# Two-layer graph network: where the joins of DMA-transposed features, tile 24's transposes and the last tile's TensorE transposes stand in their queues

## The chip, the cores and the metric

The kernel runs on one core of a Trainium2 chip. The metric is the device time of one execution in microseconds. Each core has a matrix engine (TensorE, "PE" in the profile, with its weight loads listed as "PEld"), a vector engine (DVE), a scalar engine (ACT), a general engine (POOL, GpSimd), and a queue that issues transfers (SP). POOL and ACT can issue transfers too. The engines run side by side; each takes its own instructions in the order in which they are queued, and they wait for one another through semaphores.

## The reference

The input is `x` (3327 nodes by 1024 features) and a weighted adjacency matrix `adj` (3327 by 3327). Two layers follow each other:

```python
# layer 0: quantised graph convolution
h = relu(layernorm(x))
support = relu(act_quant(h) @ weight_quant(w0))          # then quantised again
x = x + adj @ act_quant(support)                         # up to scales
# layer 1: graph attention with 8 heads of 64 features
h = relu(layernorm(x))
Wh = h @ W                                               # 1024 -> 8 x 64
e = leaky_relu(e_src[:, None] + e_dst[None, :])          # e_src = Wh.a1, e_dst = Wh.a2
att = softmax(where(adj > 0, e, -9e15))                  # per head, over neighbours
h = elu(att @ Wh)
x = x + mlp(h)                                           # four dense layers, relu between
```

## The kernel before

The nodes are padded to 26 tiles of 128 (`T` = 26). Five stages follow one another on TensorE.

**Supports** (up to about 126 us): layer 0's quantised products, left in SBUF as 26 tiles `s_int`.

**Aggregation** (about 126 to 904 us, the loop at L798). For each tile `t` of output rows, 26 column tiles of the transposed adjacency are multiplied with `s_int`. To keep float32 accuracy with two single-pass products, each piece is split: ACT copies the rounded high part (`hi`, L191), DVE subtracts it from the original (`lo`, L195) and writes the mask byte (`mk`, L196). The 26 column tiles come in seven parts (`PARTS`: five of four tiles, two of three). `at`, `hi` and `lo` have three buffers each, so a split waits until PE has finished with the part three places earlier. A generator, `columns`, emits the loads and splits two parts ahead of the products: when the loop is at part `n` of tile `t`, the latest split emitted is part `n + 2`, which for `n` = 5 is the first part of the next tile.

When a tile's products are done, ACT takes them out of PSUM (`y`, L845, held in the name `emptied`), DVE scales them (L846, `resumed`), adds `x`, takes the layer norm's statistics and writes the normalised `y` (L150). Then the features have to be transposed for `Wh = h @ W`. `transposed_by_dma` (L613) splits the float32 words into 16-bit halves: ACT packs half of the columns (`yh`, L622), a DMA transpose on SP's queue turns them (`yht`, L624), and the same again for the other half. These two transfers are called planes. Then ACT puts the 16-bit halves together again, one copy for each plane (`ht`, L628, the list `joins`). The next adjacency row's first load and the next `x` tile are issued on SP behind the last plane (`issue_after(turned.ins)`, L186 and L801).

Every second tile multiplies the transposed features of two earlier tiles, `t - 2` and `t - 1`, with the head weights. Seven half-size products (L702) are combined by additions (Strassen's scheme); `combined` (L666) makes the sums before them on DVE at part 3 and `pair_of_heads` (L686) threads the products in between those of parts 5 and 6. `closing_of_heads` (L763) then makes scores and features: score sums on DVE, `ratio` and two `ft` exponentials on ACT (L776, L780), the feature product on DVE (L781), and the feature's split into three bfloat16 terms `fw` (ACT L785, DVE L786, ACT L787, DVE L788). `fw` has one buffer; it is written to `feat_d` in HBM by POOL's queue (L791). `rows_of_scores` (L746) transposes the source scores and sends them to `src_d`. The engines' queues are ordered by a scheduler from the program; `queue_behind(a, b)` (L155) puts `a` behind `b` there without a semaphore.

**Hand-over** (about 904 to 962 us). The last two tiles have no pair of their own in the loop. Tile 24 goes through `heads` (L731), eight matmuls on the DMA-transposed `ht`, with its output in the one `sp` bank of PSUM, taken out by ACT (`wht`, L743). Tile 25 is transposed by PE itself (`transposed_by_tensor`, L637): two groups of four transposes, "turns", both into the one PSUM bank `last`, each taken out by an ACT copy (L648). Both tiles keep their own features for head 0 in SBUF (`own`, L790, `f_even`). The attention's first groups are threaded in between by the list `turn` (L1060).

**Attention** (to about 1876 us). For each head and each of four node ranges, ACT makes `over` (L953: is source plus destination score positive), DVE turns it with the mask into two fp8 selections `sel` (L962, L963), and PE sums the features over all 26 tiles (`acc`, L982). The 13 pairs of tiles form seven groups (`GROUPS`); pair 6 has its `over` from DVE. `over` has two buffers, `sel` six; selections are made two groups ahead. The score row `srow` (L917), masks (L908) and features (L902) come by SP's queue.

**Dense layers** end the kernel, the first of them threaded into the last attention row.

The lines of the hand-over that are changed read:

```python
        queue_behind(planes[0], load_src(0))
        with tc.issue_after(turned.ins):
            ins = load_features(0, range(8))
        ...
        queue_behind(joins[0], ends["scalar"])
        queue_behind(joins[1], joins[0])
        queue_behind(emptied, joins[1])
        queue_behind(resumed, ends["vector"])
        select(1)
        turn = [(of_k[-1], turns[0][0]), (turns[-1][1], last_of_k[0]), (last_of_k[-1], None)]
```

Here `planes`, `joins`, `emptied` and `resumed` hold what the last pass through them left: the planes and joins of tile 24, `y` and its scaling of tile 25. `ends` are the first and last ACT instruction and the last DVE instruction of the first selection.

Of the kernel before, what the change touches and what calls it, by code (L numbers as in the profile page):

```python
# [67 lines left out]
def two_layer_kernel(  # L68
# [23 lines left out]
    nc = tc.nc  # L92
# [81 lines left out]
    with tc.tile_pool(name="at", bufs=2, reuse_waits="tile") as atp:  # L174
# [3 lines left out]
        def adjacency(t, js, mk, turned):  # L178
# [11 lines left out]
            hi = atp.tile([P, PN, P], F32R, tag="hi", name="hi", bufs=3)[:, :nj]  # L190
            ins = nc.scalar.copy(hi, at)  # L191
            if t == 0:
# [8 lines left out]
            if js is PARTS[-1]:  # L201
                if t == T - 1:
                    nc.vector.memset(mk[:, :, rows_of(t) :], EDGE)
                nc.gpsimd.dma_start(mask_d[t], mk)
            return hi, lo, mk

        def adjacencies():
            for t in range(T):
                mk = None
                for js in PARTS:  # L210
                    hi, lo, mk = adjacency(t, js, mk, turned)
                    yield hi, lo
# [383 lines left out]
        with tc.tile_pool(name="differences", bufs=1, reuse_waits="tile") as dp, tc.tile_pool(  # L596
# [16 lines left out]
            def transposed_by_dma(y, t):  # L613
# [6 lines left out]
                for c in range(FC):  # L620
# [3 lines left out]
                    planes.append(nc.sync.dma_start_transpose(yht, yh.rearrange("p two f -> p (two f)")))  # L624
                    parts.append(yht)
                for c, yht in enumerate(parts):
                    joins.append(
# [6 lines left out]
                    )  # L634
                return ht, planes[-1]

# [25 lines left out]
            def weight_differences():  # L662
                for d, one, other in ((t3, b22, b12), (b12, b12, b11), (t2, b22, b12), (t4, b21, t2)):
                    nc.vector.tensor_tensor(d, one, other, ALU.subtract)
# [133 lines left out]
            for t in range(T):  # L798
# [6 lines left out]
                for n, js in enumerate(PARTS):  # L805
# [7 lines left out]
                    if t == 1 and n == 0:  # L813
                        weight_differences()
                    if paired and n == 3:
                        of = combined(t - 2)
# [35 lines left out]
                if t == T - 1:  # L852
                    break
                ht, turned = transposed_by_dma(y, t)
                hts[t], scales[t] = ht, r
# [25 lines left out]
    with tc.tile_pool(name="over", bufs=2, reuse_waits="tile") as overp, tc.tile_pool(  # L881
# [156 lines left out]
        load_mask(0, slice(0, TH), nc.gpsimd)  # L1038
        queue_behind(planes[0], load_src(0))
        with tc.issue_after(turned.ins):  # L1040
            ins = load_features(0, range(8))
        with tc.issue_after(ins.ins):
# [11 lines left out]
        ends = select(0)  # L1054
        queue_behind(joins[0], ends["scalar"])
        queue_behind(joins[1], joins[0])
        queue_behind(emptied, joins[1])
        queue_behind(resumed, ends["vector"])
        select(1)
        turn = [(of_k[-1], turns[0][0]), (turns[-1][1], last_of_k[0]), (last_of_k[-1], None)]  # L1060
        closed = None
# [314 lines left out]
```

## Time and profile before

| | |
|---|---|
| median of 3 runs | 2143.02 us (2140.07 to 2144.79) |
| profiled execution | 2139.64 us |
| its span, first to last instruction | 2137.9 us |
| mean granted TensorE clock | 0.997 |
| PE busy | 2089.6 us (98%) |
| ACT busy, DVE busy | 1335.8 us (62%), 1471.2 us (69%) |
| PE's waits, 126 to 905 us | 9.0 us in 14 places |
| DMA engines, 900 to 960 us | share 0.99 to 1.12, 221 to 402 GB/s |

The profile is of one execution. A row of a timeline gives the start, the duration, the engine, the source line, the operation with its output and inputs, and in brackets how long the engine had been idle before it and which instruction ended that. A row of waits gives who waited for whom, the total in us, how many times, and the longest. `SPq` is SP's queue of transfers; its durations are those of issuing. TensorE's clock falls after idle time, so an idle PE costs more than the gap: in the window 905 to 915 us the granted clock is 0.66.

### The profile page before, as it was taken

To read this page: it belongs to the slowest core of one execution; us is meant where nothing else is said; L and a number is where in the kernel's file an instruction comes from. 1 tells how busy PE (TensorE), PEld (TensorE's weight loads), DVE (VectorE), ACT (ScalarE), POOL (GpSimd) and SP (SyncE) were. 2 spreads that over 40 slices of the span, in tenths; PEclk is the share of its full clock that TensorE was granted. 3 is DMA by queue.
4 is the path that set the end of the run, shared out by engine and by line. 5 is a ranking of instruction groups with operands and counts; after the bars stand their busy time and mean duration, and the time that the engine had idled before them with its cause. 6 is when DMAs were issued, how large, how long until landed. Compare 5 with 4: busy or idle time off the path is not lost.

```text
span 2137.9 us, 37932 instructions
## 1 busy us (share of the span) xinstructions
PE 2089.6 (98%) x15387; PEld 1743.2 (82%) x15397; DVE 1471.2 (69%) x2884; ACT 1335.8 (62%) x1814; POOL 171.9 (8%) x251
## 2 busy tenths in 40 slices
PE   5999999999999999999999999999999999999999
PEld 2468888778788888779999999999999999844444
DVE  8845677666666776667777777777777777645446
ACT  6734455444444554478888888888898888742321
POOL 2300000000020000200000000000000000000000
PEclk9999999999999999999999999999999999999999
DMA  6644655545456654591202102020212004443322
GB/s 218 174 148 126 169 164 151 140 127 142 138 155 169 164 151 141 162 338 30 68 23 70 26 25 74 19 73 22 74 25 74 25 18 130 112 109 126 107 91 74
DMA packets 195471, 233.82 MB, mean 109 GB/s; under 512 B 105188, under 2 KB 140084, under 8 KB 195296
## 3 DMA queue, kind: packets, MB, share of 16 engines
q1 hardware_dynamic: 179916, 176.92, 29.3%
q0 software_dynamic: 15312, 54.42, 8.9%
q8 instruction: 120, 1.97, 0.4%
q14 instruction: 55, 0.45, 0.1%
q10 hardware_dynamic: 68, 0.06, 0.0%
HBM read 141.74 MB, written 66.02 MB: 97 GB/s over the span
## 4 chain that ended last, share of the span: by engine, by line
PE 80%; DVE 8%; DMA 5%; ACT 4%; issue 3%; POOL 0%; DVEq 0%; SPq 0%; ACTq 0%; POOLq 0%
PE acc L982 41%; PE mm L824 18%; PE o L1286 7%; PE products L702 6%; PE h_ps L1218 5%; PE mm L345 3%; DMA yht<-yh 2%; ACT over L953 1%; DMA feat_d<-fw 1%; DVE ft L781 1%; DVE prod L770 1%; ACT ht L628 1%; DVE lo L195 1%; DVE fw L788 1%; DVE stats L147 1%
## 5 line engine op out<-in xcount | busy, mean ns | idle before, releaser
L982 PEld LDWEIGHTS <-sel 128*128 128x128 fp8e4 x10816 | 933.5, 98 | 6.8 <-issue 4.8
L953 ACT ACTIVATE over<-srow,large_dst 128x896 uint8<-128x896 f32 (+1 forms) x766 | 684.5, 975 | 31.9 <-DVE sel L962 30.4
L982 PE MATMUL acc<-f_even,sel 128*128 128x195 bf16 x5408 | 470.0, 248 | 1.2 <-ACT wht L743 0.7
L982 PE MATMUL acc<-f_odd,sel 128*128 128x195 bf16 x5408 | 467.4, 247 | 0.0
L824 PE MATMUL mm<-s_int,lo 128*128 128x512 f32 x1352 | 431.7, 396 | 5.0 <-DVE lo L195 4.9
L824 PE MATMUL mm<-s_int,hi 128*128 128x512 f32 x1352 | 427.7, 398 | 4.1 <-ACT hi L191 4.1
L962 DVE TENSOR_TENSOR sel<-over,mask 128x448 uint32<-128x448 uint32 (+1 forms) x416 | 243.8, 586 | 213.0 <-ACT over L953 117.6
L824 PEld LDWEIGHTS mm<-s_int,lo 128*128 128x128 f32 x1352 | 253.6, 188 | 61.8 <-DVE lo L195 9.8
L824 PEld LDWEIGHTS mm<-s_int,hi 128*128 128x128 f32 x1352 | 253.9, 188 | 58.2 <-ACT hi L191 6.4
L963 DVE TENSOR_TENSOR sel<-sel,mask 128x448 uint32<-128x448 uint32 (+1 forms) x416 | 245.9, 591 | 14.2
L191 ACT CAST hi<-at 128x512 fp32r<-128x512 f32 (+1 forms) x182 | 105.5, 586 | 125.4 <-PE mm L824 92.1
L195 DVE TENSOR_TENSOR lo<-at,hi 128x512 fp32r<-128x512 f32 (+1 forms) x182 | 117.7, 647 | 47.9 <-ACT hi L191 47.9
L1030 POOL DMA_DIRECT2D enc_d<-eh x64 | 57.7, 905 | 860.4 <-ACT eh L1028 859.9
L1001 DVE TENSOR_REDUCE su<-acc 128x130 f32<-128x390 f32 x208 | 115.6, 556 | 7.9 <-PE acc L982 7.9
L1015 ACT ACTIVATE ht<-su,rs 128x64 f32<-128x64 f32 x208 | 53.1, 335 | 108.6 <-DVE rs L1011 108.6
L1228 ACT ACTIVATE h<-h_ps,rest 128x512 f32<-128x512 f32 (+1 forms) x52 | 33.7, 655 | 118.7 <-PE h_ps L1218 118.7
L628 ACT COPY ht<-yht 128x1024 uint16<-128x1024 uint16 x50 | 67.3, 1348 | 56.7 <-DMA yht<-yh 56.5
L345 PE MATMUL mm<-w_int,xqt 128*128 128x512 bf16 x406 | 93.5, 383 | 6.9 <-DVE w_int L476 4.5
L622 ACT COPY yh<-y 128x1024 uint16<-128x1024 uint16 x50 | 51.9, 1038 | 68.5 <-DVE y L150 68.5
L345 PEld LDWEIGHTS <-xqt 128*128 128x128 bf16 x416 | 40.5, 99 | 55.1 <-issue 8.8
L196 DVE TENSOR_SCALAR mk<-at 128x512 uint8<-128x512 f32 (+1 forms) x182 | 72.4, 398 | 0.0
L781 DVE TENSOR_TENSOR ft<-wht,ft 128x512 f32<-128x512 f32 x52 | 33.6, 689 | 50.4 <-ACT ft L780 50.3
(248 smaller groups left out, 1968.8 us busy)
## 6 DMA issues: line engine op xcount, KB each, us to landing
at<-in_adj_t SPq DMA_DIRECT2D x130, 256.0 KB, 3.1
feat_d<-fw POOLq DMA_DIRECT2D x26, 780.0 KB, 7.7
x_d<-xt POOLq DMA_DIRECT2D x26, 512.0 KB, 4.0
nodes<-x_d SPq DMA_DIRECT2D x26, 512.0 KB, 4.8
xt<-in_x SPq DMA_DIRECT2D x25, 512.0 KB, 4.1
out<-yo SPq DMA_DIRECT2D x50, 256.0 KB, 2.0
xs<-in_x SPq DMA_DIRECT2D x24, 512.0 KB, 4.4
mask_d<-mk POOLq DMA_DIRECT2D x26, 416.0 KB, 3.8
```

Source lines behind the costliest of these rows:

```text
L191: ins = nc.scalar.copy(hi, at)
L195: low = nc.vector.tensor_tensor(lo, at, hi.bitcast(F32), ALU.subtract)
L345: nc.tensor.matmul(mms[t][:, r], xqts[t][:, k, :], w_int[:, k, r], start=(k == 0), stop=(k == KF - 1))
L702: nc.tensor.matmul(ps, st[:, k], mv[:, k], start=(k == 0), stop=(k == KF // 2 - 1))
L824: nc.tensor.matmul(mm[:, c * 512 : (c + 1) * 512], which[:, q, :], s_int[j][:, c * 512 : (c + 1) * 512], start=(j == 0 and which is hi), s ...
L953: nc.scalar.activation(over[:, q], srows[i], AF.Relu, bias=large_dst[:, j, h : h + 1], scale=BIG)
L962: pin(nc.vector.tensor_tensor(up, over, of_pair, ALU.bitwise_and))
L963: ends["vector"] = pin(nc.vector.tensor_tensor(dn, up, of_pair, ALU.bitwise_xor))
L982: ins = nc.tensor.matmul(accs[i, b][:, r], chosen[i, pair][:, s, b, q], f[:, j, r], start=(j == 0 and s == 0), stop=(j == T - 1 and s == 1),)
L1001: nc.vector.tensor_reduce(su[:, b], accs.pop((i, b)).rearrange("p (q s c) -> p q c s", q=2, s=3), AX.X, ALU.add)
L1218: ins = nc.tensor.matmul(pss[m][:, :cols], wt[:, k, m * P : (m + 1) * P], xt[:, k, :cols], start=(k == 0), stop=(k == k_n - 1),)
L1286: nc.tensor.matmul(ps, st[:, k, q // 2], mv[:, k], start=(k == 0), stop=(k == 1))
```

## The change

Three things are moved; no arithmetic is added or taken away.

1. The joins leave `transposed_by_dma` and are emitted later, by `join_planes`: at part 3 of an even tile, at part 5 of an odd one. The first join is queued behind the latest split (`highs[-1]`) that has been emitted by then: part 5 of the tile in an even one, the next tile's part 0 in an odd one, and part 6, the last there is, in tile 25. The second join is not tied to the first except for tile 24, where a line for it remains. In the queue that results, the second plane's join of an odd tile stands ahead of the first's: behind the split of part 6, with one `fw` copy and the next tile's first split between the two.
2. The score row of the first attention range is queued behind tile 24's last plane instead of in front of its first one, and the first features behind the score row. `y` of tile 25 is queued behind the first selection's `over`s, which are queued behind the joins; before, the joins stood behind those `over`s and `y` behind the joins.
3. The last tile's turns, which stood together behind the first attention group, are put in two places: four transposes behind the first group, four behind the second. Tile 25's head products move from behind the second group to behind the third.

On POOL, tile 23's features are issued after two score rows instead of three. On DVE in the hand-over two more selections stand ahead of tile 24's feature product.

```diff
@@ adjacency, adjacencies
-            ins = nc.scalar.copy(hi, at)
+            ins = high = nc.scalar.copy(hi, at)
...
-            return hi, lo, mk
+            return hi, lo, mk, high
+
+        highs = []
...
-                    hi, lo, mk = adjacency(t, js, mk, turned)
+                    hi, lo, mk, high = adjacency(t, js, mk, turned)
+                    highs.append(high)
                     yield hi, lo
@@ transposed_by_dma
                     parts.append(yht)
+                return ht, planes[-1], parts
+
+            def join_planes(ht, parts):
+
                 for c, yht in enumerate(parts):
                     joins.append(
                         nc.scalar.copy(
...
-                return ht, planes[-1]
@@ the loop over tiles
+                    if t > 0 and n == (3 if paired else 5):
+                        join_planes(ht, parts_of_ht)
+                        queue_behind(joins[0], highs[-1])
...
-                ht, turned = transposed_by_dma(y, t)
+                ht, turned, parts_of_ht = transposed_by_dma(y, t)
@@ hand-over
-        queue_behind(planes[0], load_src(0))
-        with tc.issue_after(turned.ins):
-            ins = load_features(0, range(8))
+        scores = load_src(0)
+        queue_behind(scores, planes[-1])
+        ins = load_features(0, range(8))
+        queue_behind(ins, scores)
...
-        queue_behind(joins[0], ends["scalar"])
         queue_behind(joins[1], joins[0])
-        queue_behind(emptied, joins[1])
+        queue_behind(ends["first"], joins[1])
+        queue_behind(emptied, ends["scalar"])
         queue_behind(resumed, ends["vector"])
         select(1)
-        turn = [(of_k[-1], turns[0][0]), (turns[-1][1], last_of_k[0]), (last_of_k[-1], None)]
+        turn = [
+            (of_k[-1], turns[0][0]),
+            (turns[0][1], turns[1][0]),
+            (turns[1][1], last_of_k[0]),
+            (last_of_k[-1], None),
+        ]
```

## The prediction

> **What bounds the kernel now.** The page first: TensorE (PE) is busy nearly throughout, so only what makes PE idle, or slow, counts.
>
> ```profile
> PE 2089.6 (98%) x15387; PEld 1743.2 (82%) x15397; DVE 1471.2 (69%) x2884; ACT 1335.8 (62%) x1814; POOL 171.9 (8%) x251
> ```
>
> Next PE's waits, from 126 to 905 us (aggregation) and from 905 to 1100 us (hand-over to attention):
>
> ```profile
> PE mm L824 <- DVE lo L195: 4.9, 10, 0.6
> PE mm L824 <- ACT hi L191: 4.1, 4, 1.8
> ```
>
> ```profile
> PE whm L738 <- ACT ht L628: 4.7, 1, 4.7
> PE tp L644 <- ACT ht L648: 2.0, 1, 2.0
> PE acc L982 <- ACT wht L743: 0.7, 1, 0.7
> ```
>
> (total us, times, longest.) 9.0 us in the first stage, 7.4 and a last 0.3 in the second. The timeline shows the cause of the first. All 14 waits lie in odd tiles, at the seventh part. Tile 23:
>
> ```profile
> 831.94 0.51 ACT L191 CAST hi<-at 128x384 fp32r<-128x384 f32 x1
> 835.66 1.35 ACT L628 COPY ht<-yht 128x1024 uint16<-128x1024 uint16 x1 [3.21 <-DMA yht<-yh]
> ...
> 839.85 1.02 ACT L191 CAST hi<-at 128x384 fp32r<-128x384 f32 x2
> ```
>
> ```profile
> 841.70 0.73 PE L824 MATMUL mm<-s_int,lo 128*128 128x512 f32 x2 [0.57 <-DVE lo L195]
> ```
>
> ACT stands at the join (the ht copy) until the DMA transpose lands; the split hi of part 6 (839.85) is behind it, and PE runs dry. The hand-over, DMA issue and PE:
>
> ```profile
> 899.36 0.33 SPq L917 DMA_DIRECT2D srow<-src_d  x1
> 899.74 4.88 SPq L624 DMA_TRANSPOSE yht<-yh  x2
> ```
>
> ```profile
> 908.70 9.47 PE L738 MATMUL whm<-whead,ht 128*128 128x512 f32 x16 [4.73 <-ACT ht L628]
> 918.01 0.85 PE L982 MATMUL acc<-f_even,sel 128*128 128x195 bf16 x8
> 919.60 4.31 PE L982 MATMUL acc<-f_even,sel 128*128 128x195 bf16 x48 [0.73 <-ACT wht L743]
> 923.74 0.60 PE L644 MATMUL tp<-ident,y 128*128 128x128 f32 x4
> 926.31 0.66 PE L644 MATMUL tp<-ident,y 128*128 128x128 f32 x4 [1.97 <-ACT ht L648]
> 926.80 6.61 PE L982 MATMUL acc<-f_even,sel 128*128 128x195 bf16 x56
> 933.25 7.05 PE L738 MATMUL whm<-whead,ht 128*128 128x512 f32 x16
> ```
>
> Tile 24's transposes were issued at 899.74 though their input was ready at 890.3 and 892.8: they stood behind the score row load (row 899.36). The same 16 head matmuls take 9.47 after the idle and 7.05 later; 56 acc matmuls take 6.61 here and 4.85 in steady state (252 in 21.85). And in the last rows PE is only just fed:
>
> ```profile
> 938.12 0.92 POOL L791 DMA_DIRECT2D feat_d<-fw  x1 [22.12 <-DVE fw L788]
> ```
>
> ```profile
> 949.80 1.07 ACT L785 CAST fw<-ft 128x1040 bf16<-128x1040 f32 x1 [5.53 <-DMA feat_d<-fw]
> ...
> 956.09 0.50 ACT L790 COPY f_even<-fw 128x390 bf16<-128x390 bf16 x1
> ```
>
> The write of tile 24's features takes 11.6 us; tile 25's split into the one fw buffer waits for it; tile 25's own features are in SBUF at 956.6, and the seventh group of row 0 needs them at about 957.5 (940.14 + 200 matmuls at 0.0867). Slack 0.9 us: this chain will cap what the hand-over gains.
>
> **What the Trainium skill says.** "TensorE: Matmul & The Clock Gate", What's actually happening: an idle window of about 3.4 us halves PE's clock until a busy one has passed. The trace agrees: after the 4.73 us head weight loads come 0.855 us apart until 913.7, then 0.43. It also shows a fall after only 2.38 us of idle near 413 (94 matmuls in 23.20 instead of 21.60 us). The same page, Architectural detail: ACT and DVE are strict FIFOs; the tile 23 rows agree. "DMA: Bandwidth & Descriptors", Queues, rings and completion order: the DMA engines alternate between queues packet by packet. That fits 11.6 us beside the mask loads against a median of 7.7.
>
> **Part 1, joins behind later splits.** Joins remain two of 1.35 us per tile; only their place changes. In an odd tile ACT's order becomes hi(5), table load, ratio, ft x2, hi(6), second plane's join, fw, hi(next 0), first join, fw, hi(next 1), hi(next 2), y. Tile 23: hi(5) ends 832.45; table load 1.28 to 833.7; ft waits for dst (DVE 835.4) to 835.7; hi(6) to 836.3; lo(6), behind DVE's ft pair (1.29), to 837.4. PE wants it at 841.13: 3.7 us early. So the 9.0 us of waits go, and the cold spell they caused in tile 9 (1.60): 10.6.
>
> New wait: the second plane's join. Its transpose's issue ends at 834.24; even tiles show landing 2.5 later (857.33 to 859.84), so 837: join 838.4, fw 839.5, DVE ft 840.8, lo(next 0) 841.5. Behind it on ACT stand fw, hi(next 0) and the first join; PE wants lo(next 0) at 841.13 + 2.72 + 0.45 = 844.3. Slack 2.8. Only tile 9 (the wait at 413), whose first plane landed at 408.5, is tight: second plane about 410.8, lo(10, 0) at 415.3 against 414.5, loss 0.8. Bounds: 0 (planes as early as in tile 23) to 4 (1 us in four tiles). I take 0.8, giving **9.8**. Even tiles: hi(5) now precedes both joins; the sums still start when the second plane has landed and joined (859.84 + 1.35): nothing, hidden by that DMA; without that cover, hi(5)'s 0.5 per tile.
>
> **Part 2, tile 24's transposes ahead of the score row.** SP's 4.88 us of two transposes and the x loads move ahead of the score row; they can issue at 891.4 and 892.8, after the last adjacency load. Slowest landing in this case is 6.0 from issue, so 898.8. Joins wait for hi(6) of tile 25 (898.4) and interleave with the fw splits: 898.4 to 902.2. Before PE's end of tile 25 (903.97). Heads start there, warm: 4.73 + 2.42 saved so far, to 911.05. Cost: feat_d of tile 23 leaves 1.3 later (first join in front of fw); no PE work waits for it. The score row still waits for the last mk (899.36), lands at 903.6; four overs to 907.4; y 1.10 to 908.4 (was 911.3); four overs 912.2; table load 913.5. DVE: y scale 908.7, x add, statistics, two sel pairs, y 914.5, lnv; lns 914.8; wht to 915.4.
>
> Here is the new wait: the second acc tile needs wht's bank. PE stops at 911.9 and resumes at 915.5 (919.60 before): 3.6 us, and by the trace's own two cases a cold spell, 1.6 to 2.4, taken as 2.0. Zero if the window misses it.
>
> **Part 3, two places for the turns.** Same eight transposes, two ACT copies of 0.56. First turn 922, group 1 to 927.1, second turn, group 2 to 932.5, heads to 939.5. The 1.97 us bank wait is hidden by group 1, as is its 1.76 us cold spell (6.61 - 4.85). With 2.43 + 2 x 4.85 more, group 6 would start at 951.6 instead of 957.1.
>
> But ACT and DVE reach feat_d(24) no earlier: copy 2 about 929.9, power and splits, write at 939 (938.12 before), since the over/sel buffers follow PE's groups. Masks and row loads start some 6 us sooner, so the write competes less: 8.5 us, between 7.0 (a free queue) and 11.6: lands 947.5. Then fw, ft, overs, fw, own copy: 5.8, at 953.3. PE waits 1.2 at group 6; end of group 6 957.8 instead of 962.0: gain **4.2**. With 11.6: 1.1; with 7.0: 5.4; with no cold spell and a fast chain: 7. I take 4.0.
>
> **Sum.** 9.8 + 4.0 = 13.8 off the profiled 2139.64 (span 2137.9 and 1.7 around it): 2125.8. The median of the runs shown is 2143.02, 3.4 higher, so **2129.3**. Behind group 6 PE has no wait over 0.3 us, so the gain carries through.
>
> **Rivals.** (A) The features' chain takes the hand-over's whole gain: only 9.8, 2133.2. For it: 11.6 us and 0.9 us of slack. Against: the mask traffic is moved forward. (B) The second plane lands late in most odd tiles: four to eight keep half a microsecond to one, cold spells with them; about 5 us gained, 2138. For: landings up to 6.0 us; against: slack 2.8 in tile 23. (C) Slower: the second plane's join blocks ACT so long in each of 12 odd tiles that hi(next 0) is later than hi(6) was. It decides from 13.8 / 12 = 1.15 us a tile, so a landing 4 us beyond the 2.5 taken; at 6 beyond, 12 x 3.2 = 38 lost, 2143 + 38 - 14 = 2167. Against: the first plane's join row would then have shown such waits in even tiles, and shows 1.2. (D) Splits held up elsewhere, no difference: 2143.
>
> **Numbers.** Mine 0.72, A 0.13, B 0.07, C 0.04, D 0.04. Mine alone spans gains of 9 to 19: 2124 to 2134. With A and run scatter (2140.07 to 2144.79 for one kernel) 8 in 10 lie in 2123.5 to 2137. About 0.2% (4.3 us) is what can be told from no change: faster 0.72 + 0.13 + 0.05 of B = 0.90, within 0.05, slower 0.05.
>
> **What would show it.** PE's waits in the aggregation at most 1.5 us; no cold spell at 415; head matmuls 7.05 directly behind tile 25; a wait of some 3 us of acc on wht; group 6's wait on the own copy. Wrong if hi(next 0) shows new waits in odd tiles, if the feature write lands over 11 us, or if transposes delay the last adjacency part.

## The result, and the profile after

The changed kernel takes 2127.58 us (median of 5 runs, 2127.30 to 2132.78), the kernel before, run beside it, 2140.07 us (5 runs). The ratio is 0.9942, with a 95% interval of 0.9925 to 0.9958: 12.5 us less. In the profiled executions the span goes from 2137.9 to 2127.1 us, 10.8 us less. The total agrees with the prediction of 2129.3 us; the two terms it is made of do not, so that the closeness is luck. (The prediction took its 13.8 us off a median of 2143.02 from three runs; the five runs give 2140.07.)

Two stretches hold the difference; the supports ahead of them took 0.8 us longer and the rest behind them 0.8 us less, which cancels. The aggregation (first to last product of `mm`) went from 777.6 us (126.36 to 903.97) to 762.2 us (127.13 to 889.36): 15.4 us gained, where 9.8 were forecast. The hand-over (from there to the transpose of the last score rows, at 961.83 before and 951.87 after) went from 57.9 to 62.5 us: **4.6 us lost**, where 4.0 were to be gained. 15.4 - 4.6 = 10.8, the difference of the spans.

The page after, engines' busy time:

```profile
PE 2084.3 (98%) x15397; PEld 1744.6 (82%) x15397; DVE 1469.5 (69%) x2884; ACT 1336.7 (63%) x1814; POOL 169.0 (8%) x251
```

PE's waits after the change: the view from 126 to 889 us lists none, and that from 887 to 1100 us these four (total, times, longest):

```profile
PE acc L991 <- ACT wht L749: 4.6, 1, 4.6
PE tp L650 <- ACT ht L654: 4.1, 1, 4.1
PE acc L991 <- ACT f_even L796: 1.9, 1, 1.9
PE whm L744 <- ACT srct L761: 1.1, 1, 1.1
```

11.7 us of waits, where the hand-over had 7.4 before. The timeline of ACT in tile 23 after the change, with the joins in their new places:

```profile
822.03 0.50 ACT L191 CAST hi<-at 128x384 fp32r<-128x384 f32 x1
822.68 1.36 ACT L635 COPY ht<-yht 128x1024 uint16<-128x1024 uint16 x1 [0.15 <-DMA yht<-yh]
...
825.54 0.62 ACT L191 CAST hi<-at 128x512 fp32r<-128x512 f32 x1 [0.57 <-DMA at<-in_adj_t]
826.06 1.35 ACT L635 COPY ht<-yht 128x1024 uint16<-128x1024 uint16 x1
```

The split of the seventh part (822.03) now stands ahead of both joins. In the prediction's rows of before, a join waited 3.21 us for the DMA transpose with that split behind it; here the join waits 0.15 us, and no wait of PE stands in this stretch.

Now the hand-over, PE's timeline after the change:

```profile
890.51 7.13 PE L744 MATMUL whm<-whead,ht 128*128 128x512 f32 x16 [1.15 <-ACT srct L761]
897.48 0.85 PE L991 MATMUL acc<-f_even,sel 128*128 128x195 bf16 x8
902.95 6.97 PE L991 MATMUL acc<-f_even,sel 128*128 128x195 bf16 x48 [4.62 <-ACT wht L749]
909.76 0.60 PE L650 MATMUL tp<-ident,y 128*128 128x128 f32 x4
910.19 5.00 PE L991 MATMUL acc<-f_even,sel 128*128 128x195 bf16 x56
919.28 1.11 PE L650 MATMUL tp<-ident,y 128*128 128x128 f32 x4 [4.09 <-ACT ht L654]
920.18 6.00 PE L991 MATMUL acc<-f_even,sel 128*128 128x195 bf16 x56
926.02 7.05 PE L744 MATMUL whm<-whead,ht 128*128 128x512 f32 x16
932.91 12.71 PE L991 MATMUL acc<-f_even,sel 128*128 128x195 bf16 x146
947.56 4.46 PE L991 MATMUL acc<-f_even,sel 128*128 128x195 bf16 x50 [1.94 <-ACT f_even L796]
```

The heads run warm and nearly at once, as foreseen. Set against the prediction, in us after the end of tile 25's products (903.97 before, 889.36 after; the prediction's own times less 903.97):

| | before | predicted | after |
|---|---|---|---|
| tile 24's heads end | 14.2 | 7.1 | 8.3 |
| PE resumes, wht's bank free | 15.6 | 11.5 | 13.6 |
| first turn | 19.8 | 18.0 | 20.4 |
| second turn (before: behind the first) | | 23.1 | 29.9 |
| tile 25's heads start | 29.3 | 28.5 | 36.7 |
| seventh group starts | 53.5 | 49.3 | 58.2 |
| score transpose | 57.9 | 53.8 | 62.5 |

The heads end 5.9 us sooner than before. Where the bank is free again 2.0 are left, and at the first turn PE is 0.6 us later than before. The largest loss against the prediction stands between the first turn and the heads of tile 25: 16.3 us instead of 10.5. That is a link which the prediction had not seen. The timeline of POOL and DVE there, first before the change and then, with ACT, after it:

```profile
913.11 1.00 POOL L758 DMA_DIRECT2D src_d<-srct  x2 [5.22 <-DMA feat_d<-fw]
...
920.22 0.69 DVE L770 TENSOR_TENSOR prod<-wht,a_t 128x512 f32<-128x512 f32 x1 [0.25 <-issue]
```

```profile
904.29 1.00 POOL L764 DMA_DIRECT2D src_d<-srct  x2 [7.97 <-DMA feat_d<-fw]
...
910.63 0.69 DVE L776 TENSOR_TENSOR prod<-wht,a_t 128x512 f32<-128x512 f32 x1 [7.29 <-DMA src_d<-srct]
...
915.14 1.98 ACT L962 ACTIVATE over<-srow,large_dst 128x896 uint8<-128x896 f32 x2 [8.52 <-DVE sel L971]
...
918.66 0.57 ACT L654 COPY ht<-tp 128x512 f32<-128x512 f32 x1
```

The second is to be read upward from its last row. The first turn's copy (918.66) stands on ACT behind `over`s that wait for a buffer, and those wait for DVE's selections. DVE stands 7.29 us in front of `prod`, though its input `wht` has been there since 902.9. `prod` shares its one buffer with `srct`, the transposed source scores of earlier tiles (tag "prod", L754 before), and two of the ten transfers that read `srct` were issued only at 904.29, after the write of tile 23's features had landed. That write was issued at 891.87 and landed 12.1 us later. The order on POOL is the same in both traces: one score transfer, the feature write, seven and then two score transfers. So it is not the number of score rows ahead of the write, named with the change above, that makes the difference.

### The profile page after: what moved, and what is told of

Read it like the earlier page. It is cut to its first block, busy times and chain, and to the rows that moved or that the text cites. A ratio compares the mean times of both kernels' runs of the same rounds, so it can differ in the third digit from the quotient of the medians.

```text
span 2127.1 us, 37945 instructions
## 1 busy us (share of the span) xinstructions
PE 2084.3 (98%) x15397; PEld 1744.6 (82%) x15397; DVE 1469.5 (69%) x2884; ACT 1336.7 (63%) x1814; POOL 169.0 (8%) x251
## 3 DMA queue, kind: packets, MB, share of 16 engines
q8 instruction: 120, 1.97, 0.4%
## 4 chain that ended last, share of the span: by engine, by line
PE 91%; DVE 3%; DMA 2%; ACT 2%; issue 2%; POOL 0%; SPq 0%; DVEq 0%; POOLq 0%; ACTq 0%
PE acc L991 41%; PE mm L833 28%; PE o L1301 7%; PE products L708 7%; PE h_ps L1233 5%; PE mm L348 3%; ACT over L962 1%; DMA feat_d<-fw 1%; PE h_ps L1159 1%; DMA xqt<-xq 0%; DMA w<-in_w 0%; DVE stats L261 0%; DMA yht<-yh 0%; ACT xb L320 0%; DVE w_stats L391 0%
## 5 line engine op out<-in xcount | busy, mean ns | idle before, releaser
L991 PEld LDWEIGHTS <-sel 128*128 128x128 fp8e4 x10816 | 935.3, 98 | 12.5 <-issue 10.5
L972 DVE TENSOR_TENSOR sel<-sel,mask 128x448 uint32<-128x448 uint32 (+1 forms) x416 | 245.9, 591 | 14.2
L1015 DVE SCALAR_TENSOR_TENSOR su<-su,ratio 128x65 f32<-128x65 f32 x208 | 59.7, 287 | 7.4
```

What stands on the lines that cost most here:

```text
L972: ends["vector"] = pin(nc.vector.tensor_tensor(dn, up, of_pair, ALU.bitwise_xor))
L991: ins = nc.tensor.matmul(accs[i, b][:, r], chosen[i, pair][:, s, b, q], f[:, j, r], start=(j == 0 and s == 0), stop=(j == T - 1 and s == 1),)
```

## The experiments

The kernel before is run beside each set; its median was 2141.28 us in the first, 2144.73 in the second and 2136.87 in the third, while the changed kernel took 2127.58 and 2127.64 us on two occasions. Each of the three sets ran on another chip. So ratios are compared within a set, and stretches of a profile across sets; where medians are set side by side across sets, the text says so. A stretch is that of one execution: the changed kernel's hand-over was 62.5 us in one profile and 61.3 in another. Where tile 24's transposes and joins are queued alike, tile 24's heads waited 0.95 to 1.15 us in four profiles (both of the change, handover_only, own_direct) and 2.50 to 3.20 in four others (own_srct, turns_together, early_wht, odd_only), in which the first join waited longer for its DMA transpose. All runs, with the two stretches in the profiled execution:

| kernel | set | median us | ratio to before, 95% interval | aggregation us | hand-over us |
|---|---|---|---|---|---|
| before | result | 2140.07 | 1 | 777.6 | 57.9 |
| the change | result | 2127.58 | 0.9942 (0.9925 to 0.9958) | 762.2 | 62.5 |
| splits_only | 1 | 2127.78 | 0.9932 (0.9920 to 0.9944) | 763.1 | 57.1 |
| handover_only | 1 | 2142.88 | 1.0007 (1.0001 to 1.0014) | 775.7 | 60.7 |
| own_srct | 1 | 2126.41 | 0.9930 (0.9918 to 0.9942) | 763.4 | 60.5 |
| turns_together | 1 | 2131.79 | 0.9956 (0.9944 to 0.9968) | 762.8 | 66.1 |
| splits_turns | 2 | 2128.49 | 0.9928 (0.9915 to 0.9942) | 763.0 | 64.0 |
| own_direct | 2 | 2124.62 | 0.9908 (0.9894 to 0.9922) | 763.0 | 56.0 |
| early_wht | 2 | 2121.82 | 0.9890 (0.9877 to 0.9904) | 763.1 | 52.6 |
| srct_first | 2 | 2120.08 | 0.9888 (0.9873 to 0.9903) | 763.6 | 51.3 |
| odd_only | 3 | 2128.24 | 0.9958 (0.9944 to 0.9971) | 762.7 | 61.8 |
| features_first | 3 | 2121.25 | 0.9930 (0.9917 to 0.9942) | 762.3 | 55.5 |
| after_again | 3 | 2127.64 | 0.9956 (0.9943 to 0.9968) | 762.5 | 61.3 |

Theory: the prediction's, that each part gains by itself. Rivals: that the hand-over's gain is eaten by the features' chain (A of the prediction), or by the new link through `srct`'s buffer.

**Part 1 alone.** Late joins; the hand-over's queues as before, with tile 24's joins behind the first selection and the turns in one place.

```diff
-                        queue_behind(joins[0], highs[-1])
+                        if t < T - 1:
+                            queue_behind(joins[0], highs[-1])
...
-        scores = load_src(0)
-        queue_behind(scores, planes[-1])
-        ins = load_features(0, range(8))
-        queue_behind(ins, scores)
+        queue_behind(planes[0], load_src(0))
+        with tc.issue_after(turned.ins):
+            ins = load_features(0, range(8))
...
+        queue_behind(joins[0], ends["scalar"])
         queue_behind(joins[1], joins[0])
-        queue_behind(ends["first"], joins[1])
-        queue_behind(emptied, ends["scalar"])
+        queue_behind(emptied, joins[1])
...
-        turn = [
-            (of_k[-1], turns[0][0]),
-            (turns[0][1], turns[1][0]),
-            (turns[1][1], last_of_k[0]),
-            (last_of_k[-1], None),
-        ]
+        turn = [(of_k[-1], turns[0][0]), (turns[-1][1], last_of_k[0]), (last_of_k[-1], None)]
```

> Part 1 alone: the joins of all tiles but 24 stand behind later splits; transposes, joins and turns of the hand-over as in the kernel before. The recorded working (aggregation gains 9.8, hand-over gains 4.0): 9.8 us under the kernel before, slower than the whole change by 4. The rival read from the two traces (aggregation 777.6 us before against 762.3 after, hand-over 58.0 against 62.6): 15.3 us under the kernel before, so 4 to 5 us faster than the whole change; PE's weight loads show no wait for hi or lo in the aggregation.

**Parts 2 and 3 alone.** Joins emitted directly behind the transposes in all tiles but the last pass; the hand-over as changed.

```diff
-                    if t > 0 and n == (3 if paired else 5):
+                    if t == T - 1 and n == 5:
                         join_planes(ht, parts_of_ht)
...
                 ht, turned, parts_of_ht = transposed_by_dma(y, t)
+                if t < T - 2:
+                    join_planes(ht, parts_of_ht)
```

> Parts 2 and 3 alone: tile 24's transposes ahead of the score row and the turns in two places, joins of all other tiles at once behind their planes as in the kernel before. The recorded working: 4.0 us under the kernel before. The rival: 4 to 5 us over it, with a DVE wait of 5 us or more at tile 24's first prod for the source scores' write, and PE's second turn late by 3 us or more.

Part 1 alone gave 0.9932, which is all of the gain, and the hand-over's parts alone 1.0007 (1.0001 to 1.0014): a cost of 1.5 us, hardly more than nothing, but no gain. Neither theory's times came out: the first kernel was 13.5 us under the kernel before, where 9.8 and 15.3 had been forecast, and the second was to be 4.0 under or 4 to 5 over it. The first was also to differ from the whole change by 4 us or more, and their medians are 2127.78 and 2127.58 us, in different sets. The aggregation went to 763.1 us with the first and to 775.7 with the second. In the timeline of the first, the hand-over keeps its old waits of PE:

```profile
895.08 9.27 PE L744 MATMUL whm<-whead,ht 128*128 128x512 f32 x16 [4.95 <-ACT ht L635]
904.18 0.86 PE L992 MATMUL acc<-f_even,sel 128*128 128x195 bf16 x8
906.55 4.31 PE L992 MATMUL acc<-f_even,sel 128*128 128x195 bf16 x48 [1.52 <-ACT wht L749]
910.70 0.60 PE L650 MATMUL tp<-ident,y 128*128 128x128 f32 x4
913.27 0.66 PE L650 MATMUL tp<-ident,y 128*128 128x128 f32 x4 [1.97 <-ACT ht L654]
913.76 5.00 PE L992 MATMUL acc<-f_even,sel 128*128 128x195 bf16 x56
```

and takes 57.1 us with all of them, 5.4 less than the hand-over that was meant to remove them. Why the medians do not show these 5.4 us is not settled: the rest of the kernel takes 1176.6 us here and 1175.3 with the change, which gives back 1.3, and this profile is of an execution of 2125.55 us, 2.2 below its median, that of the change of one 1.4 above. The second kernel shows the new waits without part 1:

```profile
903.72 7.13 PE L744 MATMUL whm<-whead,ht 128*128 128x512 f32 x16 [0.95 <-ACT srct L761]
...
916.80 5.75 PE L993 MATMUL acc<-f_even,sel 128*128 128x195 bf16 x48 [5.26 <-ACT wht L749]
...
931.81 1.11 PE L650 MATMUL tp<-ident,y 128*128 128x128 f32 x4 [3.98 <-ACT ht L654]
```

So they come from parts 2 and 3 and not from the later joins in the tiles before. The hand-over's cost is thus 1.5 us by the medians of this set and 2.8 by its profile (60.7 against 57.9 us).

**The buffer of `srct`.** The whole change, and `srct` in another buffer that is free by then.

```diff
-                srct = s2.tile([P, EMB], F32, tag="prod", name="srct", bufs=1)[:, :P]
+                srct = s2.tile([P, EMB // 2], F32, tag="u2", name="srct", bufs=1)[:, :P]
```

> The whole change, but the transposed source scores (srct) lie in the buffer of u2 instead of prod's, so that tile 24's prod no longer waits for their write to HBM. If that wait is what turned the hand-over's gain into a loss: the wait of 7.3 us at prod and the 4.1 us at the second turn go, with the slow clock behind it (1.2 + 0.5), so 5 to 6 us under the whole change if the features' chain comes as much earlier, 2 us at least. If the loss is the wait for wht and its cold spell alone: no difference to the whole change beyond 1 us.

**The turns in one place.** Parts 1 and 2, without part 3.

```diff
-        turn = [
-            (of_k[-1], turns[0][0]),
-            (turns[0][1], turns[1][0]),
-            (turns[1][1], last_of_k[0]),
-            (last_of_k[-1], None),
-        ]
+        turn = [(of_k[-1], turns[0][0]), (turns[-1][1], last_of_k[0]), (last_of_k[-1], None)]
```

> Parts 1 and 2 without part 3: the last tile's eight transposes together behind the first group. The recorded working: the second four wait 2 us for the bank again and cost a cold spell of 1.8, so 2 to 4 us over the whole change. The rival (the copy of the first four is held up on ACT by selections that DVE delays at prod): the wait at the second turn is then longer than 4 us since nothing is in front of it, 8 us or more, and the run 4 us or more over the whole change, less what the features' chain hides.

With its own buffer for `srct`, `prod` no longer waits (`wht` ends at 905.41):

```profile
905.75 0.68 DVE L776 TENSOR_TENSOR prod<-wht,a_t 128x512 f32<-128x512 f32 x1
```

The second turn has no wait either. In the other four kernels that have part 2 and the shared buffer (turns_together, odd_only, handover_only, after_again) `prod` waited 5.94 to 6.85 us for these transfers. But the time fell by little, to 2126.41 us, between the two expectations, and the hand-over is still 2.6 us longer than before: the next link was ready. The timeline of this kernel, ACT and PE:

```profile
939.17 1.07 ACT L791 CAST fw<-ft 128x1040 bf16<-128x1040 f32 x1 [4.69 <-DMA feat_d<-fw]
...
944.43 0.50 ACT L796 COPY f_even<-fw 128x390 bf16<-128x390 bf16 x1
...
944.99 6.08 PE L991 MATMUL acc<-f_even,sel 128*128 128x195 bf16 x50 [3.76 <-ACT f_even L796]
```

The wait on tile 25's own features doubled to 3.76 us, and cooled PE: 50 products in 6.08 us instead of 50 x 0.0867 = 4.33. The heads here also waited 3.17 us for `srct`'s copy, against 1.15, and ran in 8.83 us, because the first join had waited 3.38 us for its transpose, against 1.26. The edit does not touch that. The late join hides part of the edit's worth.

With the turns in one place the second turn waits for the same late copy with no group to cover it:

```profile
920.87 1.12 PE L650 MATMUL tp<-ident,y 128*128 128x128 f32 x4 [9.12 <-ACT ht L654]
```

The hand-over takes 66.1 us against 62.5 and 61.3, and the kernel 2131.79 us against the 2127.58 and 2127.64 of the whole change in other sets. Beside part 2, part 3 is thus worth about 4 us by both; the ratios, 0.9956 here and 0.9942 and 0.9956 for the whole change, do not separate them.

**Part 3 beside part 1.** Turns in two places, tile 24's transposes behind the score row as before.

```diff
@@ against part 1 alone
-        turn = [(of_k[-1], turns[0][0]), (turns[-1][1], last_of_k[0]), (last_of_k[-1], None)]
+        turn = [
+            (of_k[-1], turns[0][0]),
+            (turns[0][1], turns[1][0]),
+            (turns[1][1], last_of_k[0]),
+            (last_of_k[-1], None),
+        ]
```

> Parts 1 and 3 without part 2: later joins, turns in two places, tile 24's transposes behind the score row as before. With part 1 alone 2127.8 us, and there the second turn waits 1.97 us for the bank; own copy of tile 25 at 942.4 us, wanted at 925.49 + 200 x 0.0867 = 942.8. Theory that the features' chain caps the hand-over: the 1.97 us go from the second turn and come back as a wait of the seventh group on the own copy, 2127 to 2128.5 us. Rival, that part 3 is a gain of its own and part 2 the loss: about 2 us less than part 1 alone, 2125 to 2126.5 us.

The second turn's wait was gone, and the seventh group waited for the own features and ran cold:

```profile
946.73 7.12 PE L992 MATMUL acc<-f_even,sel 128*128 128x195 bf16 x50 [3.46 <-ACT f_even L796]
```

The median is 0.7 us above part 1 alone, in another set, and the ratio the same within its interval: no gain. The second copy of the turns stood at 919.92 instead of 914.06, and tile 24's exponentials are queued behind it (`queue_behind(power, copies[-1])`), so the write of tile 24's features was issued at 929.43 instead of 923.83, and tile 25's split behind it. Part 3 moves its own gain onto the features' chain, as in the prediction's rival A. Not all of the delay is part 3's: already the first turn came 23.4 us after tile 25's end instead of 20.6, behind a wait of 0.98 us for the first features and one of 2.36 for `wht` that part 1 alone did not have or had shorter (1.52).

**The own features without the chain.** The whole change, `srct` in its own buffer, and tile 25's own features made from `ft` directly, ahead of the split that waits for `fw`.

```diff
+                if t == T - 1:
+                    of_0 = own[:, t].rearrange("p (q s c) -> p q s c", q=2, s=3)
+                    rest = s2.tile([P, EMB // 2], F32, tag="p1", name="rest", bufs=1)[:, : 2 * HC]
+                    rest = rest.rearrange("p (q c) -> p q c", q=2)
+                    nc.scalar.copy(of_0[:, :, 0], ft[:, 0])
+                    nc.vector.tensor_tensor(rest, ft[:, 0], of_0[:, :, 0], ALU.subtract)
+                    second = nc.scalar.copy(of_0[:, :, 1], rest)
+                    nc.vector.tensor_tensor(of_0[:, :, 2], rest, of_0[:, :, 1], ALU.subtract)
...
-                nc.scalar.copy(fw[:, :, :, 0], ft)
+                split = nc.scalar.copy(fw[:, :, :, 0], ft)
+                if t == T - 1:
+                    queue_behind(split, second)
...
-                if own is not None:
+                if own is not None and t < T - 1:
```

> The whole change, with the source scores' copy in a buffer of its own (2126.4 us, where the seventh group waited 3.76 us for tile 25's own features and then ran 50 products in 6.08 us instead of 4.33), and the own features of tile 25 made straight from ft, in four small instructions that need neither fw nor the write of tile 24's features. Theory that the features' chain caps the hand-over: that wait and its cold spell go, 5.5 us less, 2120 to 2122 us. Rival, that selections come too late there in any case, because ACT stands at the fw split: the wait changes its name to sel, 2125 to 2127 us.

**`wht` earlier**, on top of that:

```diff
-            queue_behind(taken, lacking)
+            queue_behind(taken, emptied)
...
-        select(1)
+        queue_behind(select(1)["first"], taken)
```

> As the kernel before it in this list, and wht of tile 24 taken directly behind y on ACT, ahead of the second selection's overs and of the table load. There PE waited 2.35 us for wht, then ran 48 products in 5.79 us instead of 4.15. If wht's place on ACT is what costs: up to 3.9 us less, 2117 to 2119 us; wait of acc on wht under 1 us. If a later link (turn copies, selections) is what sets the end: within 1 us of the kernel before.

**`srct`'s copy and tile 23's `fw` splits ahead of the joins**, on top of both:

```diff
-                nc.scalar.copy(srct[:n], sp[:n, :P])
+                copied = nc.scalar.copy(srct[:n], sp[:n, :P])
...
+        queue_behind(joins[0], copied)
         queue_behind(joins[1], joins[0])
```

> As the kernel before it in this list, and the copy of the source scores and both fw splits of tile 23 ahead of tile 24's joins on ACT, instead of between and behind them. If the heads wait for the sp bank behind those splits: heads start about 2 us earlier, 2115 to 2117 us. If the landing of the transposes is what counts: the wait is then on the join, under 1 us less.

The first of the three took the wait away altogether; its timeline of PE behind the heads of tile 25 is one unbroken row:

```profile
929.13 17.01 PE L1001 MATMUL acc<-f_even,sel 128*128 128x195 bf16 x196
```

196 x 0.0867 = 17.0: no wait on own features, no cold spell. Its hand-over is 56.0 us against 60.5 in own_srct. The time expected was 2120 to 2122 us and the median was 2124.62. Two things go some way to explain that: the heads ran 2.4 us earlier than in own_srct but `wht` came no more than 0.6 earlier (PE resumes at 904.85 against 905.46), so that PE waited 5.87 us instead of 2.35 and then ran 48 products in 7.00 us instead of 5.79; and behind the hand-over there is a wait of 0.91 us (of `acc` for DVE's `su`, which empties the first accumulators).

```profile
904.85 7.00 PE L1001 MATMUL acc<-f_even,sel 128*128 128x195 bf16 x48 [5.87 <-ACT wht L749]
```

The second shows what the place of `wht` costs:

```profile
902.84 5.25 PE L1001 MATMUL acc<-f_even,sel 128*128 128x195 bf16 x56
```

All 56 products of the first group in one row, no wait: 52.6 us, 2121.82. That is 2.8 us less than the kernel before it in this list; up to 3.9 less, and 2117 to 2119 us, had been expected; the heads waited 3.20 us for `srct` here, against 1.15, and ran in 8.83 us. `wht` was taken as soon as they ended, at 903.04. The third starts the heads directly behind tile 25 and then finds the next link:

```profile
889.97 7.03 PE L744 MATMUL whm<-whead,ht 128*128 128x512 f32 x16
900.70 6.61 PE L1002 MATMUL acc<-f_even,sel 128*128 128x195 bf16 x56 [3.70 <-DMA f_even<-feat_d]
```

It took 1.3 us off the hand-over and 1.7 off the median; 2115 to 2117 us had been expected, and its interval overlaps that of the kernel before it, so a gain in time is not shown. The heads' early start is in the trace and mostly lost to the next wait, for the first features. It is the fastest kernel of this study: 2120.08 us, ratio 0.9888 (0.9873 to 0.9903). A shorter hand-over gives back a little later on: behind it these three kernels wait 0.91 to 1.65 us for `su`, and the rest of the kernel takes 1176.6 to 1177.4 us against 1175.3 in the changed one.

**The load in front of the score row.** The last kernel, with the first features' load moved.

```diff
-        queue_behind(scores, planes[-1])
-        ins = load_features(0, range(8))
-        queue_behind(ins, scores)
+        features = load_features(0, range(8))
+        queue_behind(features, planes[-1])
+        queue_behind(scores, features)
+        ins = scores
```

> The last kernel of the list before this one (source scores' copy in a buffer of its own, own features of tile 25 direct, wht early, score copy ahead of the joins: ratio 0.9888), where PE then waited 3.70 us for the first features of the attention (f_even from feat_d) and ran 56 products in 6.61 us instead of 4.85; here their load is issued in front of the score row, not behind it. If the load's place on SP decides: the wait shrinks by up to 1.7 us and the clock holds, 2 to 3 us less, ratio 0.9875 to 0.9885. If its buffer or the mask loads beside it decide: no gain, and with the score row later up to 2 us more, 0.989 to 0.990.

A miss: the hand-over grew from 51.3 to 55.5 us, and the median is 2121.25 against 2120.08 us (in another set; the expected ratios were 0.9875 to 0.9885 or 0.989 to 0.990, and 0.9930 lies above both, beside a kernel before that was faster in this set). The score row pays for it, on ACT:

```profile
899.05 3.84 ACT L973 ACTIVATE over<-srow,large_dst 128x896 uint8<-128x896 f32 x4 [9.04 <-DMA srow<-src_d]
```

The row is issued at 885.98 instead of 886.42, and lands 13.1 us later instead of 6.4; PE then waits 5.74 us for the first selection. In these two profiles the order of the two loads decides which of them PE waits for, and the score row first is the better order. From 880 to 940 us the DMA engines are at a share of 0.98 to 1.17 in them; that what is left of the hand-over's waits is a matter of transfers fits this, and no run tests it.

**Which joins.** The whole change, with the even tiles' joins where they stood.

```diff
-                    if t > 0 and n == (3 if paired else 5):
+                    if t > 0 and not paired and n == 5:
                         join_planes(ht, parts_of_ht)
...
                 ht, turned, parts_of_ht = transposed_by_dma(y, t)
+                if t % 2:
+                    join_planes(ht, parts_of_ht)
```

> The whole change, with the joins of even tiles where they stood before (emitted directly behind the transposes); only those of odd tiles are late. The aggregation took 777.6 us before and 762.3 after the change, 15.3 less, where PE's waits name only 10.6 with their cold spell. Theory, that the waits in odd tiles cost more than PE's rows show: even tiles give nothing, the aggregation takes 762 to 763 us and the time is that of the change, ratio 0.993 to 0.995. Rival, that the other 4.7 us came from the even tiles, where the first split behind the joins got earlier: 766 to 768 us, ratio 0.996 to 0.997.

> The changed kernel as it is, on the same chip as the other two: ratio 0.993 to 0.996. If the later joins alone (0.9932) are as good as the whole change, it lies at or above 0.9932; below 0.992 the hand-over's two parts would be a gain after all.

The aggregation took 762.7 us with the odd tiles' joins alone and 762.5 with all of them; ratios 0.9958 and 0.9956. The even tiles give nothing, and all of the 15 us come from the odd ones. The traces of the kernel before and of the changed one agree: the even tiles from 2 to 24 take 35.93 to 35.98 us before and 35.94 to 35.96 after, the odd ones from 3 to 23 take 24.01 to 28.09 before and 23.57 to 23.74 after. The ratio of the first lies above its expected 0.993 to 0.995, but so does that of the whole change beside it; the stretch is what tells the theories apart. The whole change lies above part 1's 0.9932; as the kernel before differs by 4.4 us between the two sets, this says no more than the medians do (2127.64 and 2127.78 us): no gain of the hand-over's two parts is seen.

## Why the prediction was right, and where it was wrong

**Part 1: right in mechanism, 9.8 us where it measured 15.4.** No wait of PE on `hi` or `lo` is left, the cold spell behind 413 us is gone, the 0.8 us residual in tile 9 did not come, and even tiles gave nothing. The term that was mis-sized is "the 9.0 us of waits go, and the cold spell they caused in tile 9 (1.60): 10.6". It took PE's rows of waits as the price. The Trainium skill, "Perfetto Trace Analysis", Tensor Engine Instruction, says that the end of a matmul in a profile is computed from its size and not observed; this trace shows what that does to a wait. The timeline of PE in tile 9, before:

```profile
410.78 0.61 PE L824 MATMUL mm<-s_int,lo 128*128 128x512 f32 x2
413.20 0.73 PE L824 MATMUL mm<-s_int,hi 128*128 128x512 f32 x2 [1.81 <-ACT hi L191]
414.51 0.74 PE L824 MATMUL mm<-s_int,lo 128*128 128x512 f32 x2 [0.57 <-DVE lo L195]
415.08 1.02 PE L824 MATMUL mm<-s_int,hi 128*128 128x512 f32 x2
```

Such pairs follow one another every 0.453 us when PE is fed (the rows ahead of these: 409.42, 409.87, 410.33, 410.78), yet each is drawn 0.61 us long, 0.16 into the next. By starts, the second row comes 2.42 us after the first and so 1.97 us late, and the third 1.31 - 0.45 = 0.86 us late; the brackets say 1.81 and 0.57. With 0.16 to 0.29 us hidden in each of 14 places, and smaller stalls not flagged at all, the sum falls short by a third. The rows of the weight loads do not overlap (each load is drawn 0.19 us long, and they follow one another every 0.23), and their waits in the profile of before came close:

```profile
PEld mm L824 <- DVE lo L195: 9.8, 11, 1.0
PEld mm L824 <- ACT hi L191: 6.4, 6, 2.2
```

16.2 us in 17 places, against the 15.4 measured; with the cold spell's 1.60 on top it would be too much. The lengths of the tiles say it best: in the profile of before, tile 1, where nothing waits, takes 23.57 us, and the eleven odd tiles from 3 to 23 take 15.7 us more in sum than eleven times that.

**Parts 2 and 3, the hand-over: wrong in sign, and the step of part 2 that failed is "no PE work waits for it".** The heads did start warm (7.13 us) and 5.9 us earlier than before, but:

- Heads at once: predicted directly behind tile 25, measured 1.15 us later. `joins` were done at 889.2, in time; the bank of `whm` is shared with the transposed scores, whose copy to `srct` stood on ACT behind both `fw` splits, until 890.45. The prediction did not list that copy among what is queued behind the joins. The kernel srct_first removed it.
- The wait on `wht`: predicted 3.6 us and 2.0 of cold spell, measured 4.62 and 2.8 (48 products in 6.97 us instead of 4.15). Predicted cause right: early_wht took it away. Its size came from the score row, foreseen 0.4 us ahead of tile 25's end and come 1.9 us behind it. It was issued 3.5 us ahead of that end, not 4.6 as before, for SP was busy until 885.61 with the two transposes (7.63 us of issuing, against the 4.88 of the row that the prediction used) and the loads of `x`; and ACT began on it 5.4 us after its issue, not 4.2.
- "feat_d of tile 23 leaves 1.3 later (first join in front of fw); no PE work waits for it." This is the step that failed. Two source score transfers waited for that write's landing, `prod` for those transfers, DVE's whole queue for `prod`, and ACT, with the copy that PE's second turn needs, for DVE. Before, that link was there too, but the last of these transfers had landed 1.3 us ahead of `wht` (918.26 and 919.55; the 0.25 us in front of `prod` there were not a wait for it). Set against tile 25's end, the write was issued 3.0 us later after the change, not 1.3, took 2.8 us longer (12.1 against 9.4), and the last transfer landed 6.7 us later, while `wht` came 2.0 us earlier: so `prod`'s input was there 7.4 us before its buffer. The own_srct run shows the link by removal. Removing it alone does not bring the forecast gain: the hand-over is 60.5 us without it, and comes below the 57.9 of before only with the own features taken off the chain as well (56.0), and with `wht` earlier (52.6).

**Part 3: the wait for the bank was to be hidden by the group in between; 4.09 us of it were left,** for the reason just given: the group took 5.0 us, and without it (turns_together) the wait was 9.12. Group 6's wait on the own copy was predicted at 1.2 us and measured 1.94, the write of tile 24's features at 8.5 us and measured 9.3: these sizes came near, though the write left 8.0 us later than foreseen, set against tile 25's end.

**The sum** came out near because the two errors cancel: 15.4 - 4.6 = 10.8 in place of 9.8 + 4.0 = 13.8. That is luck; with the hand-over as forecast the gain would have been 19.4.

**Rivals.** A, that the features' chain eats the hand-over's gain: true as a mechanism, and it decides as soon as the other waits are gone (own_srct, splits_turns, and own_direct by removal); but in the changed kernel its own wait was 1.94 of the 11.7 us, and the chain itself was late through DVE. Its price, 2133.2 us, rested on a first part of 9.8 us. B and C, second planes that land late: no such wait in any odd tile. D, no difference: no.

Left open: why the kernel before varies from set to set (2136.87 to 2144.73 us) while the changed one, 2127.58 and 2127.64, does not. Its aggregation was 777.6 us in one profile and 775.7 with the same joins in another, so its stalls, which hang on the landing of transfers, may be what varies. The chips differ from set to set as well; no run here was made to tell the two apart.

## What to carry to other kernels

Price a stall of the matrix engine from the starts of its rows, from the length of a repeated unit against one that does not wait, or, more roughly, from the waits of its weight loads; its own wait rows leave out what the drawn ends cover. When something is moved forward in a queue, follow each thing it delays to its end, also through buffers that are shared by tag and through other engines' queues: a write "nobody waits for" held two transfers, which held a buffer, which held an engine, which held a bank. And where several chains end at about the same time, removing one shows the next; the gain comes when the last of them is moved.

## What the runs showed of the hardware that was not expected

The score row landed 6.4 us after its issue when it was ahead of a feature load, and 13 us after when it was 0.6 us behind it. With its place next to one other load its landing time doubled, in one profile of each (srct_first and features_first). The same feature write took 12.1 us for tile 23, beside feature and mask loads, and 9.3 us for tile 24, both in the changed kernel.

PE cooled after idle times shorter than the window of about 3.4 us that the Trainium skill, "TensorE: Matmul & The Clock Gate", What's actually happening, gives. Acc products after a wait of 2.35 and 2.36 us ran at 48 in 5.79 and 5.91 us instead of 4.15, in own_srct and splits_turns. The head products ran in 7.13 us after 2.50 us in turns_together, as good as warm. Waits of 1.94 to 2.00 us cost 0.16 us or less in the new runs (48 in 4.31 after 2.00 in odd_only, 56 in 5.00 after 1.97 in splits_only), yet in the kernel before a wait of 1.97 us was followed by 56 in 6.61. So here the measurement departs from the page's figure: the same idle time can cost 1.7 us or next to nothing, and a forecast can only give both ends. (The "2.38 us of idle near 413" of the prediction are two waits, 1.81 and 0.57, with products between; four pairs behind them came 0.85 us apart instead of 0.45.)
